# A two-block attention and FFN kernel: a division as its own stage in the second attention, first loads in another order, and slot fills in separate steps

## The chip, the cores and the metric

The kernel runs on one core of a Trainium2 chip. The core has TensorE (PE in the profile; PEld is its weight load, which overlaps the matmuls), VectorE (DVE), ScalarE (ACT), GpSimd (POOL) and SyncE (SP), each with its own instruction queue that runs in order. The engines work on SBUF; PE writes its results to PSUM, from where DVE or ACT copies them to SBUF. The metric is the device time of one execution in microseconds (us), and less is better.

## The reference, cut to what matters

Four layers, each added to x. All is float32; x has 8 x 256 rows of 256, the context 8 x 256 rows of 192.

```python
x = x + _L0_xattn_ref(_layernorm(x), ctx_768, mask, Wq, Wk, Wv, Wo)       # 16 heads of 16
x = x + _L0_ffn_ref(_layernorm(x), gamma, slot_gamma, slot_embeds, w1, b1, w2, b2)
x = x + _L1_xattn_ref(_layernorm(x), ctx_768, w_q, w_k, w_v, w_out, b_out) # 16 heads of 64
x = x + _L1_ffn_ref(_layernorm(x), W_r, W_k, W_v, mu_r, mu_k)

# both attentions: softmax of q k^T over the context's 256 rows, times v, projected back
# _L0_ffn: soft mixture of experts, 8 experts of 128 slots
xn, sn = rmsnorm(x, gamma), rmsnorm(slot_embeds, slot_gamma)
logits = einsum('bnd,esd->bnes', xn, sn)
dispatch, combine = softmax(logits, over n), softmax(logits, over e and s)
slots = einsum('bnd,bnes->besd', xn, dispatch)
out = einsum('bmd,bnm->bnd', gelu(slots @ w1 + b1) @ w2 + b2, combine)
```

## The kernel before, in words

One program builds all instructions in a written order, and a scheduler puts them into the five queues. Matmuls and transposes made through the helpers `matmul` (L73) and `transpose` (L76) keep their written order on PE; other instructions may be moved within their engine. Every dependence becomes a wait on a semaphore. PSUM is split into two large tiles ("big", for scores), three of one bank ("mm", for nearly everything else) and one "o".

**Loads and prologue of the first attention.** ScalarE's queue issues wk, the mask, cq and wq; SyncE's queue issues the first 512 columns of the context (`load_ctx`), x in four pieces of 512 rows (`load_x`), wv, the rest of the context, wo in eight pieces, the slot embeddings `se`, small tensors and the first expert's weights. The landing of a DMA is told by one of eight semaphores in turn, so a DMA can only be issued once the one eight before it has landed. DVE forms `anyk` (does a batch have any key), the two scalars of the key rows, the key rows themselves (`krows`, L280), and the layer-norm statistics of all 16 tiles of x (`ln_pair`, L128 to L132). Then come the first keys (`keys0`), the transposed tokens (`tokens0`) and the first queries (`queries0`).

**First attention.** A loop over 76 steps h: each issues the scores of one query block (for the row maxima, `NM`, L459) and, six steps later, those of one key block (for the exponentials, L470), then whatever a table `whole` holds for that step: keys, values, queries of later batches, `key_rows(p)` at steps 2, 18 and 34, projections, and `slot_sum(e)` at steps 1 to 4, which squares and sums the slot embeddings (`sq` L297, `ssq` L298).

**Routing inside it.** For the first two batches the mixture's routing is also spread over the steps, by two written plans. In a plan "F57.01" means: at step 57 call `fill(0, 1)`, which multiplies the dispatch weights `dt` (kept in the tile `wq`) with x and writes the slots (L717); P, T, U, S, D are the other parts, D being the transposes into `dt`.

**Experts** follow (L933, L949), with the routing of later groups between them.

**Second attention.** 64 steps, one for each batch b and pair of heads t, run in 32 groups of two over "ticks" n. Before, a step has these stages: scores with maxima, exponentials and division (`scores` and `norm`, in one stage), `transposes` of the exponentials (copied to `et`, L1204), `values` (copied to `ot` in every second step, L1223), and at the end of a batch `project` (L1236). `norm` takes the reciprocal of the sums on DVE (L1186) and multiplies on POOL (L1188). The order of a tick is written out:

```python
for n in range(len(groups) + 4):
    b, i = n // 4 + 1, n % 4
    stage(2, n - 3)                     # values
    if b < B:
        for piece in projs[b][1][i]:    # x transposed (i = 0), then queries
            piece()
    stage(3, n - 4)                     # project
    stage(1, n - 2)                     # transposes
    ...                                 # keys (i < 2) or values' projection of a later batch
    stage(0, n)                         # scores and division
```

The queries' copy out of PSUM (`QT`, L1110) and half of that of keys and of values are on DVE, the others on ACT. During the ticks DVE also takes the statistics of the last layer (`ln_half`), and ACT their square root, which needs another function table than the exponentials.

**Last layer**: a pipeline of mix, keys and values over the 8 batches (L1333 and on).

Of the kernel before, what the change touches and what calls it, by code (L numbers as in the profile page):

```python
# [8 lines left out]
F32 = mybir.dt.float32  # L9
# [5 lines left out]
P = 128  # L15
# [47 lines left out]
def kernel(ctx: ExitStack, tc: tile.TileContext, a: dict, out: bass.AP):  # L63
# [38 lines left out]
    make_identity(nc, ident)  # L102
    nc.gpsimd.memset(epsb, EPS)

    def load_x(p):
        nc.sync.dma_start(
            x_sb[:, 4 * p : 4 * p + 4, :],
            a["x"][512 * p : 512 * (p + 1), :].rearrange("(t p) d -> p t d", p=P),
        )

    def ln_half(half, name):
# [8 lines left out]
        nc.vector.reciprocal(rstd, rstd)  # L120
        return mv, rstd

    def ln_pair(p, name):

        mv = stat.tile([P, 4, 2], F32, tag="mvp", bufs=4, name=f"mvp_{name}")
        for i in range(4):
            st = stat.tile([P, 6], F32, tag="bst", bufs=4, name=f"bst_{name}_{i}")
            nc.vector.bn_stats(st, x_sb[:, 4 * p + i, :])  # L128
            nc.vector.bn_aggr(mv[:, i, :], st)
        rstd = stat.tile([P, 4], F32, tag="rstdp", bufs=4, name=f"rstdp_{name}")  # L130
        nc.scalar.activation(rstd, mv[:, :, 1], AF.Sqrt, bias=epsb)
        nc.vector.reciprocal(rstd, rstd)  # L132
        return mv, rstd

    def moe_mean(g):

# [82 lines left out]
    with ExitStack() as l0:  # L219
# [3 lines left out]
        def load_ctx(p):  # L223
# [3 lines left out]
            for h in range(2):  # L227
                nc.sync.dma_start(ctx1T[64 * h : 64 * h + 64, cols], a["ctxT"][P:C, cols])

        wk = w0.tile([P, 2, 512], F32, name="wk")  # L230
        nc.scalar.dma_start(wk[:, 0, :], a["wk0"][0:P, :])
        for h in range(2):
            nc.scalar.dma_start(wk[64 * h : 64 * h + 64, 1, :], a["wk0"][P:C, :])
        load_ctx(0)
        load_x(0)
        maskb = w0.tile([P, B * S], U8, name="maskb")
        nc.scalar.dma_start(maskb, a["mask"].partition_broadcast(P))
        cq = w0.tile([P, 1], F32, name="cq")
        nc.scalar.dma_start(cq, a["cq"])
        wq = w0.tile([P, 2, 512], F32, name="wq")  # L240
        nc.scalar.dma_start(wq, a["wq0"].rearrange("(c p) f -> p c f", p=P))
        wv = w0.tile([P, 2, D], F32, name="wv")
        nc.sync.dma_start(wv[:, 0, :], a["wv0"][0:P, :])
        for h in range(2):
            nc.sync.dma_start(wv[64 * h : 64 * h + 64, 1, :], a["wv0"][P:C, :])
        for p in range(1, 4):
            load_x(p)
        for p in range(1, 4):
            load_ctx(p)

# [1 line left out]
        for j in range(4):  # L252
# [9 lines left out]
        nc.sync.dma_start(b1, a["b1"])  # L262


        nc.vector.tensor_reduce(
            anyk, maskb.rearrange("p (b k) -> p b k", b=B), AX.X, ALU.max
        )


        krows = w0.tile([P, B * S], F32, name="krows")  # L270
        kscale = stat.tile([P, B], F32, tag="kscale", bufs=1, name="kscale")
        kshift = stat.tile([P, B], F32, tag="kshift", bufs=1, name="kshift")
        ones = stat.tile([P, 1], F32, tag="kones", bufs=1, name="kones")
        nc.vector.tensor_reduce(ones, ident[:, HD0 + 1 : P : 32], AX.X, ALU.add)
        nc.vector.tensor_scalar(kscale, anyk, cq, BIG, ALU.mult, ALU.mult)
        nc.vector.tensor_scalar(kshift, kscale, -1.0, ones, ALU.mult, ALU.add)

        def key_rows(p):
            for b in (2 * p, 2 * p + 1):
                nc.vector.tensor_scalar(  # L280
                    krows[:, S * b : S * (b + 1)],
                    maskb[:, S * b : S * (b + 1)],
                    kscale[:, b : b + 1],
                    kshift[:, b : b + 1],
                    ALU.mult,
                    ALU.add,
                )

        key_rows(0)
        qscale = stat.tile([P, B], F32, tag="qscale", bufs=1, name="qscale")  # L290
        nc.vector.tensor_scalar(qscale, anyk, HD0**-0.5, None, ALU.mult)

        ssq = stat.tile([P, E], F32, tag="ssq", bufs=1, name="ssq")

# [98 lines left out]

        def tokens0(b):
            xT = tos[b]["xT"] = p0.tile([P, 2, S], F32, tag="xT", bufs=2, name=f"xT0_{b}")
            mv, rstd = stats0[b // 2]
            pt = transposed(normed(b, mv, rstd, "l0", of=4), f"x0_{b}", transpose)
            nc.scalar.copy(xT, pt)

        def queries0(b, t2):  # L400
# [148 lines left out]
        def at(h, f):  # L549
            whole.setdefault(h, []).append(f)  # L550

        stats0 = [ln_pair(0, "l0_0")]
        tos += [{} for b in range(B)]
        keys0(0, 0)()
        tokens0(0)
        queries0(0, 0)
        at(0, lambda: keys0(0, 1))
        at(1, lambda: queries0(0, 1))
        at(1, lambda: tokens0(1))
# [4 lines left out]
        for p in range(1, 4):  # L564
# [11 lines left out]
            at(h + 15, lambda b=b: queries0(b + 1, 1))  # L576
            at(h + 17, lambda b=b: values0(b))
            at(h + 25, lambda b=b: values0(b + 1))
        stats0 += [ln_pair(p, f"l0_{p}") for p in range(1, 4)]

        for e in range(E):
            at(1 + e // 2, lambda e=e: slot_sum(e))
# [143 lines left out]

        for b, plan in enumerate(
            (
                "P47 T48.00 T49.01 U51.0 T52.10 T53.11 S54.0 U55.1 S55.1 D56.0 F57.00 F57.01 "
                "D58.1 F60.10 F61.11",  # L730
                "P59 T63.00 T64.01 T65.10 U66.0 T68.11 S68.0 U69.1 S69.1 D70.0 F71.00 F72.01 "
                "D73.1 F74.10 F75.11",
            )
        ):
            does = dict(zip("PTUSDF", routing0(b)))
            for step in plan.split():
                when, _, args = step[1:].partition(".")
                at(int(when), lambda f=does[step[0]], args=args: f(*map(int, args)))
# [292 lines left out]
    with ExitStack() as l1:  # L1031
# [116 lines left out]
        def steps1(b, to):  # L1148
# [4 lines left out]
            for t in range(8):  # L1153
# [3 lines left out]
                def scores(t=t, tag=tag, st=st):  # L1157
                    sc = ps_big(f"sc_{tag}").rearrange("p (h q k) -> p h q k", h=2, q=2)
                    for qb in range(2):
                        for i in range(2):  # L1160
                            r = slice(64 * i, 64 * i + 64)
                            matmul(
                                sc[:, i, qb, :],
                                lhsT=to["QT"][r, t, qb * P : (qb + 1) * P],
                                rhs=to["KT"][r, t, b % 2 * S : (b % 2 + 1) * S],
                                start=True,
                                stop=True,
                            )
                    nm = stat.tile([P, 2, 2], F32, tag="nm1", bufs=4, name=f"nm_{tag}")
                    nc.vector.tensor_reduce(nm, sc, AX.X, ALU.max, negate=True)  # L1170
                    ex = p1.tile([P, 2, 2, S], F32, tag="ex", bufs=6, name=f"ex_{tag}")
                    z = stat.tile([P, 2, 2], F32, tag="z1", bufs=4, name=f"z_{tag}")
                    for qb in range(2):
                        for i in range(2):
                            nc.scalar.activation(  # L1175
                                ex[:, i, qb, :],
                                sc[:, i, qb, :],
                                AF.Exp,
                                bias=nm[:, i, qb : qb + 1],
                                accum_out=z[:, i, qb : qb + 1],  # L1180
                            )
                    st["ex"], st["z"] = ex, z

                def norm(tag=tag, st=st):
                    rz = stat.tile([P, 2, 2], F32, tag="rz1", bufs=4, name=f"rz_{tag}")
                    nc.vector.reciprocal(rz, st["z"])  # L1186
                    ex = st["ex"].rearrange("p h q k -> p (h q) k")
                    nc.gpsimd.tensor_tensor(  # L1188
                        ex,
                        ex,  # L1190
                        rz.rearrange("p h q -> p (h q)").unsqueeze(2).to_broadcast([P, 4, S]),
                        ALU.mult,
                    )

                def transposes(tag=tag, st=st):
                    et = p1.tile([P, 2, 2, S], F32, tag="et", bufs=4, name=f"et_{tag}")
                    for i in range(2):
                        pt = ps_mm(f"pe_{tag}_{i}").rearrange("p (c q) -> p c q", c=2)
                        for qb in range(2):
                            for c in range(2):  # L1200
                                transpose(
                                    pt[:, c, qb * P : (qb + 1) * P],
                                    st["ex"][:, i, qb, c * P : (c + 1) * P])
                        nc.vector.tensor_copy(et[:, i, :, :], pt)  # L1204
                    st["et"] = et

                def values(t=t, tag=tag, st=st):
# [29 lines left out]
                        x_sb[:, 2 * b : 2 * b + 2, :], po, x_sb[:, 2 * b : 2 * b + 2, :], ALU.add  # L1237
                    )

                
                def normed_scores(scores=scores, norm=norm):
                    scores()
                    norm()

                steps.append(
                    [normed_scores, transposes, values] + ([project] if t == 7 else [])
                )
            return steps

# [16 lines left out]
                piece()  # L1266
        for n in range(len(groups) + 4):
            b, i = n // 4 + 1, n % 4
            stage(2, n - 3)
            if b < B:  # L1270
                for piece in projs[b][1][i]:
                    piece()
            stage(3, n - 4)
            stage(1, n - 2)


            if i < 2 and n // 8 < B // 2 - 1:
# [165 lines left out]
```

## Time and profile before

| what | us |
|---|---|
| median of 3 runs | 1390.77 (1390.14 to 4721.38) |
| time of the profiled execution | 1386.11 |
| its span, first to last instruction | 1384.2 |
| PE busy | 1324.9 |
| first load of the function table on ACT for the exponentials | 46.6 to 47.9 |
| end of the last attention's projection | about 1326 |

Times in the profile are from the span's start. A group's row has the line, the engine, the operation, output and inputs by their names in the program, shapes and a count; then its busy time, the mean in ns of one, and the idle time of the engine just before them with what ended most of it. A row of the timeline has its start, its duration and the like; the number in brackets is how long the engine was idle before, and what released it. A row of waits has the engine and what it waited for, then the total in us, how often, and the longest. PE's granted clock over the span is 0.990 of full speed; it is lower in the first 25 us, and for some us near 215, 1240 and 1330. DMA moves 86.83 MB, a mean of 63 GB/s.

### The profile page before, as it was taken

Reading aid. Unit: us, or ns where it says so; the run is one execution under the profiler, and the core shown is the slowest. Engines: PE = TensorE matmul, PEld = TensorE weight load, DVE = VectorE, ACT = ScalarE, POOL = GpSimd, SP = SyncE. Lnnn points to the kernel's source line nnn. Section 1 sums busy time; section 2 is a strip of 40 time slices with the busy share of each in tenths; the row PEclk is TensorE's granted clock in tenths of the full one; section 3 lists DMA queues with packets and bytes.
Section 4 is the critical chain, followed back from the end, with each engine's and each line's share of the span. In section 5 each row is a group of like instructions: output and inputs, shape, how many; then the busy total and the mean of one; then the engine's idle time right before and its main releaser. Section 6 shows DMA issues by size and latency. Waiting matters only on the chain.

```text
span 1384.2 us, 18931 instructions
## 1 busy us (share of the span) xinstructions
PE 1324.9 (96%) x7504; PEld 959.3 (69%) x7504; DVE 612.0 (44%) x1223; ACT 543.8 (39%) x1320; POOL 194.9 (14%) x149
## 2 busy tenths in 40 slices
PE   5999998899999999999999999999999999999988
PEld 2566665477778876787867888856666666567667
DVE  6777776523330233322333110036655555655654
ACT  1445453545432262523534232214433433533433
POOL 1000001101010010100101000013332332332414
PEclk8999999999999999999999999999999999999999
DMA  8000000023325231332332435230000000000011
GB/s 259 13 1 1 1 2 1 1 95 130 102 93 193 65 129 65 130 130 76 118 115 79 130 129 168 72 114 0 1 0 1 1 1 0 1 1 1 1 31 54
DMA packets 58375, 86.83 MB, mean 63 GB/s; under 512 B 3248, under 2 KB 47664, under 8 KB 58288
## 3 DMA queue, kind: packets, MB, share of 16 engines
q1 hardware_dynamic: 57424, 84.33, 18.8%
q10 hardware_dynamic: 864, 1.31, 0.3%
q8 instruction: 59, 0.97, 0.3%
q14 instruction: 28, 0.23, 0.1%
HBM read 83.53 MB, written 2.10 MB: 62 GB/s over the span
## 4 chain that ended last, share of the span: by engine, by line
PE 79%; ACT 9%; DVE 7%; issue 2%; POOL 1%; DMA 1%; ACTq 0%; SPq 0%; POOLq 0%; DVEq 0%
PE ph L933 16%; PE pe L949 16%; PE sc L73 7%; ACT ex L1175 6%; PE po L73 5%; PE k L73 5%; PE q L73 4%; PE v L73 4%; PE pc L975 4%; PE o L73 3%; PE pf L879 3%; PE ln L797 3%; PE pe L76 2%; DVE nm L1170 2%; PE pf L73 1%
## 5 line engine op out<-in xcount | busy, mean ns | idle before, releaser
L933 PE MATMUL ph<-slots,w 128*128 128x256 f32 x1024 | 267.6, 385 | 0.8 <-ACT ht L941 0.2
L941 ACT ACTIVATE ht<-ph,b 128x256 f32<-128x256 f32 x256 | 119.2, 474 | 372.3 <-PE ph L933 372.0
L949 PE MATMUL pe<-w,ht 128*128 128x256 f32 x1024 | 263.8, 381 | 0.0
L933 PEld LDWEIGHTS ph<-slots,w 128*128 128x128 f32 x1024 | 182.1, 189 | 55.3 <-ACT ht L941 22.8
L949 PEld LDWEIGHTS pe<-w,ht 128*128 128x128 f32 x1024 | 192.0, 190 | 29.9 <-DVE slots L958 4.2
L1188 POOL TENSOR_TENSOR ex<-ex,rz 128x1024 f32<-128x1024 f32 x64 | 120.0, 1894 | 249.8 <-DVE rz L1186 230.7
L1175 ACT ACTIVATE ex<-sc,nm 128x256 f32<-128x256 f32 x256 | 117.4, 484 | 64.4 <-DVE nm L1170 55.7
L470 ACT ACTIVATE ex<-sc 128x512 f32<-128x512 f32 x128 | 74.8, 597 | 82.9 <-PE sc L73 76.5
L73 PE MATMUL sc<-KT,QT 17*128 17x256 f32 (+1 forms) x1024 | 105.2, 383 | 0.9 <-ACT QT L414 0.9
L958 DVE TENSOR_TENSOR slots<-pe,b 128x512 f32<-128x512 f32 x32 | 22.1, 692 | 183.5 <-PE pe L949 183.5
L459 DVE TENSOR_REDUCE NM<-sc 128x2 f32<-128x512 f32 x128 | 86.8, 688 | 32.7 <-PE sc L73 28.2
L73 PE MATMUL q<-xT,wq 128*128 128x256 f32 x384 | 94.8, 395 | 1.6 <-ACT V L1140 0.9
L73 PEld LDWEIGHTS sc<-KT,QT 17*128 17x128 f32 (+1 forms) x1024 | 78.1, 189 | 23.2 <-issue 13.4
L73 PEld LDWEIGHTS q<-xT,wq 128*128 128x128 f32 x384 | 70.9, 192 | 26.5 <-issue 11.0
L857 POOL TENSOR_TENSOR es<-es,zs 128x1024 f32<-128x1024 f32 x12 | 22.7, 1894 | 445.8 <-DVE zs L856 445.8
L76 PE MATMUL pe<-ident,ex 128*128 128x128 f32 x512 | 70.9, 280 | 13.1 <-DVE QT L1110 9.4
L1204 DVE COPY et<-pe 128x512 f32<-128x512 f32 x128 | 79.8, 677 | 1.9 <-PE pe L76 1.8
L1170 DVE TENSOR_REDUCE nm<-sc 128x4 f32<-128x1024 f32 x64 | 75.3, 1218 | 5.0 <-PE sc L73 1.3
L76 PEld LDWEIGHTS pe<-ident,ex 128*128 128x128 f32 x512 | 56.8, 142 | 27.0 <-POOL ex L1188 11.8
L73 PE MATMUL po<-wo,ot 128*128 128x256 f32 x320 | 72.6, 382 | 0.0
L73 PEld LDWEIGHTS po<-wo,ot 128*128 128x128 f32 x320 | 60.1, 190 | 11.3 <-issue 3.6
L73 PE MATMUL o<-et,V 128*64 128x256 f32 x512 | 62.8, 386 | 0.8 <-ACT ot L1223 0.8
(183 smaller groups left out, 1590.0 us busy)
## 6 DMA issues: line engine op xcount, KB each, us to landing
w<-in_w_dram SPq DMA_DIRECT2D x64, 1024.0 KB, 6.9
b<-in_b_dram SPq DMA_DIRECT2D x32, 128.0 KB, 6.7
x_sb<-in_x_dram SPq DMA_DIRECT2D x4, 512.0 KB, 6.2
out_dram<-y SPq DMA_DIRECT2D x8, 256.0 KB, 2.1
ctx0T<-in_ctxT_dram SPq DMA_DIRECT2D x4, 256.0 KB, 7.4
ctx1T<-in_ctxT_dram SPq DMA_DIRECT2D x8, 128.0 KB, 6.5
se<-in_slots_dram SPq DMA_DIRECT2D x1, 1024.0 KB, 5.7
wq<-in_wq_dram SPq DMA_DIRECT2D x1, 1024.0 KB, 4.8
```

The lines of the kernel that those rows point to most:

```text
L73: tc.keep_in_program_order(nc.tensor.matmul(out, lhsT=lhsT, rhs=rhs, start=start, stop=stop))
L76: tc.keep_in_program_order(nc.tensor.transpose(out, in_, ident))
L459: nc.vector.tensor_reduce(NMs[(2 * b + t // 2) % 2][:, qb, t, HD0 + 1 + 64 * i : 64 * i + 64 : 32], sc[i][:, :, 0, :], AX.X, ALU.max, nega ...
L470: nc.scalar.activation(ex[:, 2 - 2 * i : 4 - 2 * i, :], sc[1 - i][:, :, 1, :], AF.Exp)
L933: nc.tensor.matmul(ph, lhsT=c_["w1"][:, c, hc * P : (hc + 1) * P], rhs=slots[e][:, c * 256 : (c + 1) * 256], start=(c == 0), stop=(c == 1),)
L941: nc.scalar.activation(ht, ph, AF.Gelu, bias=b1[:, e, hc : hc + 1])
L949: nc.tensor.matmul(c_["pe"][:, b, :], lhsT=c_["ht"][hc][:, b * SL : (b + 1) * SL], rhs=c_["w2"][:, hc, :], start=(hc == 0), stop=(hc == HI ...
L975: nc.tensor.matmul(pc[:, :D], lhsT=CT[:, bl, e, t * P : (t + 1) * P], rhs=eos[e][:, bl, :], start=(e == 0), stop=(e == E - 1),)
L1170: nc.vector.tensor_reduce(nm, sc, AX.X, ALU.max, negate=True)
L1175: nc.scalar.activation(ex[:, i, qb, :], sc[:, i, qb, :], AF.Exp, bias=nm[:, i, qb : qb + 1], accum_out=z[:, i, qb : qb + 1],)
L1188: nc.gpsimd.tensor_tensor(ex, ex, rz.rearrange("p h q -> p (h q)").unsqueeze(2).to_broadcast([P, 4, S]), ALU.mult,)
L1204: nc.vector.tensor_copy(et[:, i, :, :], pt)
```

## The change

It has three parts.

In the second attention the division by the sums Z (`norm`) is a stage of its own between scores and transposes: it is written one tick after its scores, behind the transposes of the group before. Of each pair of copies to `et`, the second goes to ACT. The sums have six buffers for four.

The first loads are split and ordered: x comes in two pieces of 256 rows (a new signature of `load_x`), wk and wq in halves of 256 columns, the mask in its first 512 bytes and the rest. A square root is written ahead of them on ACT. The statistics of x are taken for the first 256 rows, then the next 256, then each 512 rows at steps 0, 1 and 2 of the loop (`ln_tiles`); `anyk`, the scalars and the query scale are formed by `key_rows` for two batches at a time. The first tokens are transposed between the two halves of the first keys.

In the plan of the first batch's routing, the second fill goes from step 57 to 58, the second transposes into `dt` from 58 to 60, and the last two fills from 60 and 61 to 61 and 62.

```diff
-    def load_x(p):
+    def load_x(n, of):
         nc.sync.dma_start(
-            x_sb[:, 4 * p : 4 * p + 4, :],
-            a["x"][512 * p : 512 * (p + 1), :].rearrange("(t p) d -> p t d", p=P),
+            x_sb[:, n : n + of, :],
+            a["x"][P * n : P * (n + of), :].rearrange("(t p) d -> p t d", p=P),
         )
-    def ln_pair(p, name):
+    def ln_tiles(n, of, name):
         mv = stat.tile([P, 4, 2], F32, tag="mvp", bufs=4, name=f"mvp_{name}")
-        for i in range(4):
+        for i in range(of):
...
-            nc.vector.bn_stats(st, x_sb[:, 4 * p + i, :])
+            tc.keep_in_program_order(nc.vector.bn_stats(st, x_sb[:, n + i, :]))
             nc.vector.bn_aggr(mv[:, i, :], st)
...
+    def ln_pair(p, name):
+        return ln_tiles(4 * p, 4, name)
...
-        load_ctx(0)
-        load_x(0)
-        nc.scalar.dma_start(maskb, a["mask"].partition_broadcast(P))
+        def load_wk(cols):
+            nc.scalar.dma_start(wk[:, 0, cols], a["wk0"][0:P, cols])
+            for h in range(2):
+                nc.scalar.dma_start(wk[64 * h : 64 * h + 64, 1, cols], a["wk0"][P:C, cols])
+        def load_mask(cols):
+            nc.scalar.dma_start(maskb[:, cols], a["mask"][cols].partition_broadcast(P))
...
+        root = stat.tile([P, 1], F32, tag="rz0", bufs=2, name="root")
+        nc.scalar.activation(root, epsb, AF.Sqrt)
+        load_x(0, 2)
+        load_wk(slice(0, 256))
+        load_ctx(0)
         nc.scalar.dma_start(cq, a["cq"])
-        nc.scalar.dma_start(wq, a["wq0"].rearrange("(c p) f -> p c f", p=P))
+        load_mask(slice(0, 512))
+        load_wq(slice(0, 256))
+        load_x(2, 2)
+        load_wq(slice(256, 512))
+        load_wk(slice(256, 512))
+        load_mask(slice(512, B * S))
...
         def key_rows(p):
+            two, tok = slice(2 * p, 2 * p + 2), slice(512 * p, 512 * (p + 1))
+            tc.keep_in_program_order(
+                nc.vector.tensor_reduce(
+                    anyk[:, two], maskb[:, tok].rearrange("p (b k) -> p b k", b=2), AX.X, ALU.max
+                )
+            )
+            nc.vector.tensor_scalar(kscale[:, two], anyk[:, two], cq, BIG, ALU.mult, ALU.mult)
+            nc.vector.tensor_scalar(kshift[:, two], kscale[:, two], -1.0, ones, ALU.mult, ALU.add)
+            nc.vector.tensor_scalar(qscale[:, two], anyk[:, two], HD0**-0.5, None, ALU.mult)
...
-        stats0 = [ln_pair(0, "l0_0")]
-        keys0(0, 0)()
+        stats0 = [ln_tiles(0, 2, "l0_0")]
+        second = keys0(0, 0)
         tokens0(0)
+        key_rows(0)
+        second()
         queries0(0, 0)
+        stats0 += [ln_tiles(2, 2, "l0_1")]
+        for p in range(1, 4):
+            at(p - 1, lambda p=p: stats0.extend([ln_pair(p, f"l0_{2 * p}")] * 2))
...
-        stats0 += [ln_pair(p, f"l0_{p}") for p in range(1, 4)]
...
-                "P47 T48.00 T49.01 U51.0 T52.10 T53.11 S54.0 U55.1 S55.1 D56.0 F57.00 F57.01 "
-                "D58.1 F60.10 F61.11",
+                "P47 T48.00 T49.01 U51.0 T52.10 T53.11 S54.0 U55.1 S55.1 D56.0 F57.00 F58.01 "
+                "D60.1 F61.10 F62.11",
...
-                    z = stat.tile([P, 2, 2], F32, tag="z1", bufs=4, name=f"z_{tag}")
+                    z = stat.tile([P, 2, 2], F32, tag="z1", bufs=6, name=f"z_{tag}")
...
-                    nc.vector.reciprocal(rz, st["z"])
+                    tc.keep_in_program_order(nc.vector.reciprocal(rz, st["z"]))
...
-                        nc.vector.tensor_copy(et[:, i, :, :], pt)
+                        (nc.scalar.copy if i else nc.vector.tensor_copy)(et[:, i, :, :], pt)
...
-                def normed_scores(scores=scores, norm=norm):
-                    scores()
-                    norm()
                 steps.append(
-                    [normed_scores, transposes, values] + ([project] if t == 7 else [])
+                    [scores, norm, transposes, values] + ([project] if t == 7 else [])
                 )
...
-            stage(2, n - 3)
+            stage(3, n - 3)
...
-            stage(3, n - 4)
-            stage(1, n - 2)
+            stage(4, n - 4)
+            stage(2, n - 2)
+            stage(1, n - 1)
```

## The prediction

> **What bounds the kernel now.** I read the engine shares first, then busy time by stage, then the waits and the gaps of TensorE (PE).
>
> ```profile
> PE 1324.9 (96%) x7504; PEld 959.3 (69%) x7504; DVE 612.0 (44%) x1223; ACT 543.8 (39%) x1320; POOL 194.9 (14%) x149
> ```
>
> ```profile
> 0.00:46.00 46.00, 30.52 (x132) 16.02 (x136) 32.22 (x98) 7.33 (x14) 3.57 (x13) 0.89 0.70 204
> 46.00:260.00 214.00, 203.57 (x1900) 125.80 (x1900) 153.12 (x310) 109.57 (x206) 13.39 (x17) 0.98 0.01 1
> 260.00:925.00 665.00, 660.06 (x2964) 511.13 (x2958) 171.09 (x377) 245.63 (x474) 31.31 (x21) 1.00 0.34 111
> 925.00:1322.00 397.00, 380.01 (x2279) 262.36 (x2278) 224.18 (x376) 157.25 (x577) 127.50 (x74) 1.00 0.00 1
> ```
>
> The rows by stage are busy times of PE, PEld, DVE, ACT, POOL, then clock, DMA share, GB/s. PE is the bound: only its idle 59 us, and its work at reduced clock, can be won. The change adds and removes no matmul. It reaches 15.5 us of idle at the start, some of the 10.4 us in the first attention, and the 17 us of the second.
>
> ```profile
> PE pe L76 <- DVE QT L1110: 9.4, 13, 2.2
> ...
> PE pe L76 <- DVE et L1204: 3.0, 4, 1.3
> PE k L73 <- DVE et L1204: 2.3, 4, 0.6
> ```
>
> ```profile
> 1034.14 0.51 ACT L1175 ACTIVATE ex<-sc,nm 128x256 f32<-128x256 f32 x1
> ...
> 1034.59 0.62 ACT L1223 COPY ot<-o 128x512 f32<-128x512 f32 x1
> 1034.84 0.18 DVE L1186 RECIPROCAL rz<-z 128x4 f32<-128x4 f32 x1 [1.65 <-ACT ex L1175]
> 1034.94 0.66 DVE L1110 TENSOR_SCALAR QT<-q 128x512 f32<-128x512 f32 x1
> ...
> 1035.74 1.16 PE L76 MATMUL pe<-ident,ex 128*128 128x128 f32 x8 [0.61 <-DVE QT L1110]
> ```
>
> The reader is to see a queue: DVE's reciprocal waits for the last exponential, QT's copy stands behind it, and the transposes wait for that copy, since q and the transposes share the three "mm" PSUM buffers.
>
> **Second attention: division as its own stage.** The reciprocal moves one tick later, behind the transposes' copies, and half of these (64 of 128) go from DVE to ACT. The reciprocal no longer waits, since its exponentials are a tick old. I count a tick from the start of values (at 1030.38). In ticks with one query piece, QT's copy can run from 3.9 to 4.6 instead of ending at 5.2, so the third transpose group finds its buffer free. The keys need the buffer of the second group, which ACT now empties: exponentials to 4.2, ot to 4.85, copy 0.6, free at 5.45, needed at 5.95. The eleven gaps of 0.61 and the first of 0.51 go: 7.2 us. In ticks that begin with pt_x, PE is at the keys by 4.6 already and ACT's copy still ends at 5.45: the four gaps of 0.57 become some 0.8, which loses 0.9. The gap at 1240 (2.17) goes with its half-speed work after it (transposes 1.75 for 1.16, scores 2.94 for 1.89): 3.8. The late gaps 0.54, 0.57, 0.56, where a copy stood behind the same reciprocal, go: 1.7. The 0.79 behind ot stays.
>
> One place gets worse: tick 20 (from 1174.8), where the FFN statistics put a square root between exponentials.
>
> ```profile
> 1176.04 1.28 ACT L1175 ACT_TABLE_LOAD   x1 [2.26 <-DVE nm L1170]
> ...
> 1180.18 0.66 PE L76 MATMUL pe<-ident,ex 128*128 128x128 f32 x4 [1.32 <-DVE et L1204]
> ...
> 1181.90 2.02 DVE L173 TENSOR_SCALAR xh_ffn<-x_sb,mv_ffn,rstd_ffn 128x256 f32<-128x256 f32 x2
> ```
>
> The exponentials there end 1.9 late, and ACT's copies stand behind them; the normalization of x (xh_ffn) now comes ahead of the V copy and the maxima. I get some 0.6 later maxima, exponentials to 1181.5, ot 1182.1, copy 1182.7, so keys start 2.0 later than their 1180.8. PE then idles some 3.3 us. Does the clock fall? The Trainium skill, "TensorE: Matmul & The Clock Gate", "HAM oscillation — how this bites in real kernels", wants no gap over about 3.4 us: by it this gap and that of 1240 cost nothing more. The trace disagrees: after 2.17 us the granted clock was 0.66 over 1240 to 1245. I take the trace: another 1.6 lost. Second attention: 7.2 + 3.8 + 1.7 - 0.9 - 2.0 - 1.6 = 8.2 us gained (by the page, at tick 20: 9.8).
>
> A second rule speaks against the move. POOL's multiplication (1894 ns, two a tick) now runs from about 5 to 9 of a tick, where half of each xh stands. Of two xh_ffn beside it, one took 1693 ns against a usual 0.4. The skill's "SBUF — State Buffer", "SBUF: two separate sides", says DVE in a two-port mode and GpSimd exclude each other for a whole instruction. So up to 1.9 us of DVE per such tick; DVE's next work there, the keys' copy, begins at 9.0, so I cost it at nothing. Without that cover the maxima and ACT would be late by as much; that is the slow rival. POOL's order also gets x + bias between two multiplications; at 5.9 us per tick in the shortest ticks its 3.8 us still fit. At the tail the last division comes some 0.9 later (POOL done at 1315.3 for 1314.4), and the second transposes start then: 0 to 0.2, taken as nothing.
>
> **First loads.** Now DVE does mask, all 16 statistics and 8 key rows before the first scores:
>
> ```profile
> 10.34 2.29 DVE L265 TENSOR_REDUCE anyk<-maskb 128x8 f32<-128x2048 uint8 x1 [10.34 <-DMA maskb<-in_mask_dram]
> ...
> 24.36 0.42 SPq L259 DMA_DIRECT2D se<-in_slots_dram  x1
> ...
> 25.65 0.71 PE L73 MATMUL sc<-KT,QT 17*128 17x256 f32 x8 [0.87 <-ACT QT L414]
> ...
> 31.36 0.75 DVE L297 TENSOR_TENSOR sq<-se 128x256 f32<-128x256 f32 x2
> ```
>
> Afterwards: x's first 256 KB land near 4.7, keys run on a cold PE (3.8 + 2.1 us by the rows at 6.01 and 9.73), the 64 KB mask waits for x's landing and comes near 10 (cq, 0.5 KB, took 4.7), key rows to 12, KT to 13.3, q and QT: first scores about 16 to 17, nine earlier. But this does not carry through. DVE then has maxima 1.3, statistics of four tiles 2.0 (0.4 + 0.17 each, a little overlapped), maxima 1.3, KT 1.2, statistics 2.0, maxima 1.3, and reaches the slot embeddings' squares (sq) near 26 to 27. Their load landed at 30.1 before (24.36 + 5.7). In DVE's new order sq still stands ahead of the second step's maxima, so the early scores wait there. The split loads put 39 DMAs ahead of it instead of 33, over eight landing semaphores; the bytes ahead are the same and the DMA engines were full (share above 1 from 5 to 20 us), so I set the landing to 31 (29 to 33). SP is moved past one more x load, ACT past five more issues of about 0.5 us; ACT has idle time there, and its table load is hidden under the first DMAs.
>
> From there to the transposes of the third x block: squares and sums 5.3, the last four statistics 1.6, maxima 3 x 1.2, mask and key rows of the second pair 1.6, QT 0.6, KT 1.2, xh 0.7, so 14.5, and 0.5 for a PE that has cooled: 46.0 against 45.27 before. A loss of 0.8, with ends of +4 (load before 26.5) and -3 (load at 33). Key rows of the third and fourth pairs, formerly in the prologue, stand in DVE's queue at steps 18 and 34, 1.8 us each (0.57 + 0.5 + 0.7), ahead of the next maxima that PE needs: between 0 and 1.8 each, I take 0.4 each: -0.8.
>
> **Slots filled in separate steps.** The rows at 222.54 (PE waits 1.31 for a slots copy) and 227.25 (0.45 for ACT's V copy) are from two fills in one step and transposes placed next to them. The new order puts scores and v between: both go, +1.8. The half-speed stretch at 213 to 219 comes from gaps before it (0.46, 0.62, 1.04, 0.24) that stay.
>
> **The sum.** 8.2 - 0.8 - 0.8 + 1.8 = 8.4 us, made against a span of 1384.2. The profiled execution took 1386.1, 4.7 below the median 1390.8 of the runs; carried to that median: 1382.4.
>
> **Rivals.** (a) The start counts: slot embeddings land before DVE wants them, and ACT keeps up in tick 20. Start +4 instead of -0.8, tick 20 without its 3.6: 1374. For it: DMA delivers up to 360 GB/s; against: the unchanged bytes ahead. (b) Nothing gained: load at 33, clock falls in two or three more gaps at 1.6 each, since the gate depends on where gaps lie: 1388 to 1391. (c) Slower: ACT becomes the bound of the copies. Its margin is 0.5 us (5.45 against 5.95); it decides as soon as maxima and exponentials come over 0.5 late, for which a DVE instruction held by POOL is enough. With 1.0 late in every tick: gaps of 0.5 in the eleven ticks (gain only 1.2), 1.8 in the four that begin with pt_x and have keys (-4.9), half of these with a fallen clock (-3.2), tick 20 -4, 1240 and the late gaps +5.5, a late load and the rest -2: 7.4 lost, 1398. With 1.9 late in each (gaps of 1.4 and 2.7, a fallen clock in all four): near 1416. For it: xh_ffn's 1693 ns; against: the cover above. (d) The change does nothing as it says: excluded by the instruction order, in which the reciprocal does move.
>
> **How the numbers follow.** Forecast 0.50 (1377 to 1387), (a) 0.27, (b) 0.13, (c) 0.10. The predicted time is the forecast's, 1382. From 1369 to 1394: below lie the better end of (a), above half of (c) and more. Over 2%, which is about what a measurement of this kernel can tell from no change, means below 1363 or above 1418.6. Below 1363 needs 28 us of some 34 within reach (17 + 1.6 in the second attention, about 12 at the start, 3.5 at the slots): 0.07 with what I may have missed. Above: the worst end of (c) and a little more, 0.03. Within: 0.90.
>
> **What would show it.** In the profile after: no wait of pe on QT; pe and the second copy on ACT; a gap ahead of k on ACT's et in pt_x ticks near 0.8, and one of about 3 us at the square root; first scores near 17, then DVE waiting for se near 27 to 31; no wait of pf on slots. Wrong, if DVE never waits for se, or if PE waits on ACT in the ticks with query pieces.

## The result, and the profile after

| | before | after |
|---|---|---|
| median, first pair of runs | 1390.45 (1387.64 to 4721.38, 4 runs) | 1375.62 (1375.34 to 1376.09, 4 runs) |
| median, repeated on another chip (e5 below) | 1387.86 (1384.71 to 1393.16, 27 runs) | 1374.75 (1373.91 to 1377.28, 6 runs) |
| profiled execution: time, span | 1386.11, 1384.2 | 1375.81, 1373.9 |

The ratio is 0.990 (95% interval 0.9881 to 0.992), and 0.9903 (0.9883 to 0.9924) in the repetition: 13 to 15 us faster, about 1%. That is under the 2% that count as a difference here, though both intervals lie clear of 1, and 6.4 us below the predicted 1382. The run of 4721 us stands alone and enters no ratio. The profiled execution of the kernel before was 4.3 us faster than its median, so the spans differ by less than the medians.

First the busy shares in the page of the kernel after, and its busy times by stage (PE, PEld, DVE, ACT, POOL, then clock, DMA share, GB/s):

```profile
PE 1326.6 (97%) x7504; PEld 961.3 (70%) x7504; DVE 575.1 (42%) x1172; ACT 578.9 (42%) x1386; POOL 194.6 (14%) x149
```

```profile
0.00:46.00 46.00, 32.27 (x121) 16.05 (x122) 29.68 (x89) 7.11 (x15) 3.56 (x13) 0.85 0.70 204
46.00:260.00 214.00, 204.33 (x1889) 125.66 (x1889) 156.99 (x328) 109.02 (x205) 12.71 (x16) 0.98 0.01 1
260.00:925.00 665.00, 660.60 (x2973) 513.63 (x2974) 170.51 (x379) 245.77 (x475) 31.90 (x22) 1.00 0.34 111
925.00:1322.00 397.00, 382.70 (x2312) 265.53 (x2310) 192.18 (x330) 195.24 (x648) 127.52 (x76) 1.00 0.01 3
```

PE is busy 1.75 us more in the first 46 us than before, but at a mean clock of 0.85 instead of 0.89: part of what it gained there is work at half speed (from 30 to 33 and from 37 to 43 us, among others). These means are not safe, though: over the first 12 us the profile states 1.00 in both, while the first key matmuls, which run then, take 3.8 us for the 2.0 of the next ones. DVE is busy 37 us less over the whole kernel and ACT 35 us more, and neither is near its limit. Fixed windows hide where time is won, because the work slides through them. So I use marks, the same event in both traces:

| mark (start of the instruction) | before | after | after, repeated | gained |
|---|---|---|---|---|
| first scores | 25.65 | 18.09 | 18.81 | 7.6, 6.8 |
| third x transposes | 45.27 | 46.90 | 46.07 | -1.6, -0.8 |
| first residual add (`x_sb<-po`) | 88.98 | 92.78 | 91.94 | -3.8, -3.0 |
| last add of the mixture (`x_sb<-pc`) | 909.99 | 912.90 | 911.08 | -2.9, -1.1 |
| last add of the second attention | 1326.03 | 1315.17 | 1313.37 | 10.9, 12.7 |

A head start of 7 us is gone 28 us later, and the second attention (from the fourth mark to the fifth) then wins 13.8 us in both executions. Its waits in the kernel after (engine and what it waited for, us in total, times, longest):

```profile
PE k L73 <- ACT et L1235: 5.1, 5, 1.7
PE o L73 <- ACT ot L1254: 0.9, 1, 0.9
PE q L73 <- ACT V L1171: 0.9, 1, 0.9
PE v L73 <- ACT et L1235: 0.8, 1, 0.8
...
```

No transpose waits for the query copy any more (9.4 us before). Instead the matmuls of keys and values wait 5.9 us for the copies that went to ACT (before, the keys waited 2.3 us for copies on DVE). At the start, rows of DVE's timeline and then of PE's (start, duration, then in brackets how long the engine stood and for what):

```profile
27.48 0.66 DVE L486 TENSOR_REDUCE NM<-sc 128x2 f32<-128x512 f32 x1
31.25 0.76 DVE L323 TENSOR_TENSOR sq<-se 128x256 f32<-128x256 f32 x2 [3.11 <-DMA se<-in_slots_dram]
```

```profile
36.21 0.77 PE L73 MATMUL sc<-KT,QT 17*128 17x256 f32 x4 [3.36 <-DVE NM L486]
37.47 1.22 PE L73 MATMUL sc<-KT,QT 17*128 17x256 f32 x4 [0.49 <-DVE NM L486]
38.62 1.12 PE L76 MATMUL nm<-ident,NM 128*128 128x128 f32 x4
39.53 1.06 PE L73 MATMUL k<-ctx0T,wk 128*128 128x512 f32 x1
```

And from PE's waits over the first 75 us:

```profile
PE sc L73 <- DVE NM L486: 4.8, 3, 3.4
```

DVE comes to the squares of the slot embeddings at 28 and stands for their load. Behind that instruction in its queue are the row maxima, and PE's scores wait 3.36 us for those. PE's rows after it show a second price: `nm` takes 1.12 us for a usual 0.66, because the clock has fallen.

### The profile page after: what moved, and what is told of

Its sections match the earlier page's. It is cut to its first block, busy times and chain, and to the rows that moved or that the text cites. A ratio compares the mean times of both kernels' runs of the same rounds, so it can differ in the third digit from the quotient of the medians.

```text
span 1373.9 us, 19006 instructions
## 1 busy us (share of the span) xinstructions
PE 1326.6 (97%) x7504; PEld 961.3 (70%) x7504; DVE 575.1 (42%) x1172; ACT 578.9 (42%) x1386; POOL 194.6 (14%) x149
## 3 DMA queue, kind: packets, MB, share of 16 engines
q1 hardware_dynamic: 57440, 84.33, 18.8%
q10 hardware_dynamic: 1584, 1.31, 0.4%
## 4 chain that ended last, share of the span: by engine, by line
PE 84%; ACT 6%; DVE 4%; DMA 2%; issue 2%; POOL 1%; SPq 0%; POOLq 0%; ACTq 0%; DVEq 0%
PE ph L964 16%; PE pe L980 15%; PE sc L73 8%; PE q L73 6%; PE o L73 5%; PE po L73 5%; PE k L73 5%; PE pc L1006 4%; PE v L73 4%; PE pe L76 4%; PE ln L828 3%; PE pf L910 3%; ACT ex L1206 2%; PE pf L73 1%; ACT ex L497 1%
## 5 line engine op out<-in xcount | busy, mean ns | idle before, releaser
L1235 ACT COPY et<-pe 128x512 f32<-128x512 f32 x64 | 37.0, 607 | 71.9 <-PE pe L76 71.5
```

## The experiments

Each experiment's median stands beside the kernel before on the same chip: 1387.16 for e1 to e4, 1387.86 for e5 to e8, 1387.19 for e9 to e12. On one chip they can be compared directly, between chips by their ratio to the kernel before.

**The parts alone (e1, e2, e3).** The kernel before with one part of the diff each: e1 the hunks of the second attention, e2 those of the loads, first statistics and key rows, e3 the routing plan.

> Before, with the second attention of the change alone (division as a stage of its own, the second copy of each pair on ScalarE, z with six buffers). Theory: all of the gain lies here and the second attention was undervalued in the prediction (8.2 us): the time falls by about 14 us, to some 1376 to 1377, below the changed kernel or level with it, and the marks of the batches' ends come 49.7 us apart instead of 51.5. Rival, the prediction's own sum: 8.2 us here, and the rest of the 14.8 us between the medians from elsewhere: 1382.

> Before, with the loads, first statistics and key rows of the change alone. Theory: the first scores start 7.5 us earlier but VectorE then stands 3 us for the slots' embeddings and TensorE's clock falls, so that nothing of the head start is left: slower than before by 3 to 4 us, about 1394. Rival (the prediction's rival a): the early start counts and something else in the changed kernel hides it: faster by 3 to 7 us, 1384 to 1387.

> Before, with the changed plan of the slots' fills alone. Theory: one wait goes (1.3 us) and another of scores for ScalarE comes, so 0 to 0.8 us faster. Rival, the prediction's sum: 1.8 us faster, if the new wait came with the later arrival at this stage and not from the plan.

Measured: e1 1375.91, ratio 0.9922 (0.9907 to 0.9937); e2 1388.87, 1.0012 (1.0001 to 1.0022); e3 1385.29, 0.999 (0.998 to 1.0). The second attention carries the gain: its stretch takes 401.8 us in e1, for 416.0 before and 402.3 after. The loads alone lose 1.7 us, half of what was expected. The plan alone wins 1.9, by the marks 1.84 at the end of the mixture. There my new theory fell and the prediction's number was right: from the first residual add to the first expert matmul the first profile of after wins only 0.4 us, but the clock over 260 to 300 us is 0.96 there; in the repetition (1.00) it wins 1.7 against e2, which has the same loads and the old plan. Over all 14 profiles of this document, from the first residual add to the end of the mixture, the six with the old plan take 820.8 to 822.3 us and the eight with the new one 819.1 to 820.2.

**Is the whole more than its parts (e5)?** The kernel after again, unchanged.

> The changed kernel as it is, beside the three below and the kernel before on one chip, because the three parts measured alone add up to about 11 us and the whole to 14.8 of medians (10.3 of spans). Theory: the parts add up and the whole is worth 11 us, a ratio of about 0.992. Rival: the parts help each other, and the ratio is again 0.990 or less.

The parts sum to 11.4 us by their medians, the whole is 13.1 here. The intervals (about 3 us) hold both, so I see no help between the parts, but a difference of 2 us could not be seen.

**The two halves of the second attention (e6, e7).** e6 has the stage of its own, e7 the copies on ACT:

```diff
 # e6: e1 with
-    (nc.scalar.copy if i else nc.vector.tensor_copy)(et[:, i, :, :], pt)
+    nc.vector.tensor_copy(et[:, i, :, :], pt)
 # e7: before with
-    nc.vector.tensor_copy(et[:, i, :, :], pt)
+    (nc.scalar.copy if i else nc.vector.tensor_copy)(et[:, i, :, :], pt)
```

> Before, with the division as a stage of its own (and six buffers of z), but both copies of each pair on VectorE as before. Theory: it is the moved reciprocal that pays, since VectorE's in-order queue stood in it for ScalarE's sums and held the copies and query copies behind it: 8 to 11 us faster, of the 11 us that both parts bring. Rival: VectorE's load is what pays (0.69 us of copy for each pair), and the stage alone brings 0 to 3 us.

> Before, with the second copy of each pair on ScalarE, but the division still behind the scores as before. Theory (the moved reciprocal pays): at most 3 us faster, or slower, because each copy on ScalarE lengthens the queue whose sums VectorE stands for. Rival (VectorE's load pays): 7 to 11 us faster.

Measured: e6 1372.19, ratio 0.9884 (0.9861 to 0.9908); e7 1385.28, 0.998 (0.9971 to 0.9989). The moved reciprocal pays, with 15.7 us even more than the 8 to 11 expected (it comes with the six buffers of the sums, which were not tried apart). Unexpected is that it pays more alone. All of PE's waits of e6 in the stretch of the second attention, and past it one of the last layer:

```profile
PE pk L1329 <- DVE xk L1315: 5.9, 1, 5.9
PE pe L76 <- POOL ex L1188: 1.6, 4, 0.8
PE q L73 <- ACT V L1140: 0.9, 1, 0.9
PE o L73 <- ACT ot L1223: 0.8, 1, 0.8
PE pe L76 <- DVE xT L1090: 0.5, 1, 0.5
```

No wait for any copy of `et` is left, though DVE makes them all; the waits for POOL's products are in the last two batches. By the marks, the copies on ACT cost and bring, on top of the stage:

| us | before | e7 copies | e6 stage | after: both |
|---|---|---|---|---|
| first batch, from the last add of the mixture | 103.79 | 103.60 | 101.32 | 102.81 |
| each of batches 1 to 3 | 51.47 | 50.95 | 49.50 | 49.71 |
| batch 4 (tick 20, feed-forward statistics) | 52.15 | 54.05 | 49.99 | 51.60 |
| batch 5 (the gap at 1240) | 48.36 | 47.28 | 43.93 | 43.52 |
| batches 6 and 7 | 57.34 | 55.64 | 57.15 | 55.21 |
| last add of the mixture to last add here | 416.0 | 413.4 | 400.9 | 402.3 |

On top of the stage they win 1.9 us at the tail and 0.4 in batch 5, and lose these and 1.4 more before: 1.5 in the first batch, 0.6 in the next three, 1.6 in batch 4. By the times alone e1 and e6 just touch in their intervals, but the marks repeat: the stretch takes 400.9 to 401.1 us in the four profiles that have the stage with all copies on DVE (e6, e9, e10, e12), and 401.8 to 403.7 in the six that have it with half of them on ACT.

**Slot sums later (e4).**

```diff
-    at(1 + e // 2, lambda e=e: slot_sum(e))
-at(5, slot_scale)
+    at(6 + e, lambda e=e: slot_sum(e))
+at(14, slot_scale)
```

> The changed kernel, with the sums of squares of the slots' embeddings at steps 6 to 13 instead of 1 to 4 and their roots at step 14 instead of 5, so that VectorE never stands for that load. Theory (VectorE's in-order queue behind this load gave the head start back): the third x transposes start some 4 to 7 us before 46.9 us, the clock between 30 and 45 us stays above .9, and the time falls by 4 to 7 us, to 1369 to 1372. Rival: another wait holds the same stretch (ScalarE's table change, the mask rows, the wait for the second half of the loads): within 1.5 us of the changed kernel.

Measured: 1374.28, ratio 0.9912 (0.9893 to 0.9931): no gain, as the rival had it. DVE still stood 1.3 us for the load, since the scheduler put the first square at 31.0. The third x transposes did come at 42.4, but the squares ended at 45.9, and their root then stood in ACT's queue with a table load behind it, ahead of the first exponentials. ACT's rows and PE's:

```profile
45.97 0.21 ACT L328 ACTIVATE ssq<-ssq 128x8 f32<-128x8 f32 x1 [2.20 <-DVE ssq L324]
46.20 1.28 ACT L497 ACT_TABLE_LOAD   x1
```

```profile
48.95 0.93 PE L73 MATMUL sc<-QT,KT 18*128 18x256 f32 x8 [2.92 <-ACT ex L497]
49.64 1.09 PE L73 MATMUL sc<-KT,QT 17*128 17x256 f32 x8
50.66 3.78 PE L73 MATMUL q<-xT,wq 128*128 128x256 f32 x8
```

Of the 4.5 us won, 2.92 turned into this wait, and in the profiled execution (1381.64; the others took 1373.2 to 1374.7) the clock stayed at half for 18 us after it, though PE was at work all along: the same query matmuls take 1.99 us at full clock. What took the rest in the other executions can't be seen, since they were not profiled.

**Slot sums on ACT (e8).** In the kernel after, ACT has nothing to do from 36.6 to 42.9 us but wait for these sums.

```diff
-    nc.vector.tensor_tensor(sq[:, 0, :], se[:, e, :], se[:, e, :], ALU.mult)
-    nc.vector.tensor_reduce(ssq[:, e : e + 1], sq[:, 0, :], AX.X, ALU.add)
+    tc.keep_in_program_order(nc.scalar.activation(
+        sq[:, 0, :], se[:, e, :], AF.Square, accum_out=ssq[:, e : e + 1]))
...
-    at(1 + e // 2, lambda e=e: slot_sum(e))
-at(5, slot_scale)
+    at(3, lambda e=e: slot_sum(e))
+at(4, slot_scale)
```

The root in `slot_scale` is kept in written order too.

> The changed kernel, with the squares of the slots' embeddings summed by ScalarE (Square with an accumulated sum, all eight at step 3, their roots at step 4) instead of by two VectorE instructions each, so that VectorE neither stands for that load nor works 6.5 us on it, and the roots are done before the first exponential. Theory: the third x transposes at 41 to 43 us instead of 46.9, no wait of the scores for VectorE over 1.5 us and none for ScalarE's exponential over 2 us before 70 us, and 4 to 6 us faster than the changed kernel on the same chip: about 1370 to 1372. Rival: the head start is lost elsewhere (a fall of the clock after other short waits): within 1.5 us of the changed kernel.

Measured: 1366.68, ratio 0.9844 (0.9819 to 0.9868), 8 us under the kernel after on the same chip, more than the 4 to 6 expected. The third x transposes start at 41.37. PE's waits in the first 75 us of e8:

```profile
...
PE sc L73 <- ACT ex L500: 2.1, 3, 1.4
PE sc L73 <- ACT QT L444: 1.5, 1, 1.5
PE sc L73 <- DVE NM L489: 0.9, 1, 0.9
```

The wait for maxima fell from 4.8 to 0.9 us. The first residual add is at 85.35, 6.6 us ahead of e5.

**The slot load earlier (e11).** The kernel after, with the load of `se` ahead of the contexts 1 to 3.

```diff
+        se = w0.tile([P, E, D], F32, name="se")
+        nc.sync.dma_start(se, a["slots"].rearrange("e s d -> s e d"))
         for p in range(1, 4):
             load_ctx(p)
```

> The changed kernel with the load of the slots' embeddings issued ahead of the contexts 1 to 3 and of wo, nothing else moved. Theory (half of the loss is VectorE standing 3 us for that load, half its 6.5 us of work on it): VectorE does not stand before the first square, the third x transposes come at about 43 to 44 us, and it is 2 to 4 us faster than the changed kernel, about 1371. Rival: the work alone counts, or the contexts arrive too late for the second keys: no faster than the changed kernel.

Measured: 1371.84, ratio 0.9892 (0.9875 to 0.9908); its interval and that of the kernel after overlap. The edit did not take the standing away: the scheduler put the first squares further forward, and DVE stood longer and earlier.

```profile
17.14 0.73 DVE L177 TENSOR_SCALAR xh_l<-x_sb,mvp_l,rstdp_l 128x256 f32<-128x256 f32 x2
21.82 0.76 DVE L323 TENSOR_TENSOR sq<-se 128x256 f32<-128x256 f32 x2 [3.94 <-DMA se<-in_slots_dram]
```

The third x transposes came at 44.71, 1.4 us ahead of e5, but the clock then fell for some 7 us (from 63 us), and the first residual add is at 92.0, as in the kernel after. So it leaves open how the loss divides between standing and 6.5 us of work.

**The best of it, and two parts taken back (e9, e10, e12).** e9 is e8 with all copies of `et` on DVE; e10 is e9 with the old loads, first statistics and key rows, e12 is e9 with the old plan.

> The changed kernel with the squares summed by ScalarE (as in the run before) and with both copies of each pair back on VectorE: the stage of the division and the loads stay. Theory (ScalarE's copies are a loss once the reciprocal has moved): the wait of the key and value matmuls for ScalarE's copy (5.6 us) goes, the batches' ends stand 49.5 us apart, 50.0 in the batch with the feed-forward statistics, and the time is 1362 to 1364. Rival: it is as fast as with the copies on ScalarE, 1366 to 1368.

> The kernel of e9 with the loads, first statistics and key rows of the kernel before. Theory: the first scores 7.5 us earlier count once VectorE is relieved, so this is slower than e9 by 3 to 6 us, about 1367. Rival: what the sums on ScalarE brought is VectorE's 6.5 us of work alone, and the loads are worth nothing: within 1.5 us of e9.

> The kernel of e9 with the plan of the slots' fills of the kernel before. Theory: the plan brings what it brought alone, so this is 1 to 2 us slower than e9. Rival: in the changed kernel the plan brought 0.6 us (a new wait for ScalarE's exponential took the rest), so within 0.8 us of e9.

Measured: e9 1365.2 (1364.15 to 1365.68), ratio 0.9838 (0.9825 to 0.9851), which beats both kernels: 22 us under before, some 9 under after. e10 1370.96, 0.988; e12 1368.11, 0.9858. The loads are thus worth 5.8 us of medians here (3.5 by the mark at the end of the mixture; their intervals don't meet), the plan 2.9 (1.9 by that mark; these intervals do meet). The copies back on DVE can't be judged by the times: e9's and e8's ratios can't be told apart. e9 lies between its theory and its rival: against e8 the second attention takes 401.1 for 403.7 us, of which 1.7 is a fall of the clock in e8's batch 4, and the first residual adds are level, since e8's fall of the clock at 28 us is the longer one and e9 has another at 59 us.

The first residual add gives a square of four for loads and sums:

| first residual add at, us | sums on DVE | sums on ACT |
|---|---|---|
| old loads | 88.98, 88.80 (e3), 88.71 (e6); 90.92 (e1), 92.47 (e7) | 88.53 (e10) |
| new loads | 92.78, 91.94 (e5), 91.98 (e2), 92.00 (e11) | 85.35 (e8), 85.62 (e9), 85.47 (e12) |

In e1 and e7 the clock rose later; beside the three other profiles, and with one profile of e10, it does not matter with the old loads who sums. With the new ones it is worth over 6 us: they win 3 us if DVE is free at that time, and lose 3 if it isn't. That the new loads win with the sums on ACT stands on the times too (e9 against e10); the loss without them is 1.7 us by the medians of e2, and by these marks no larger than the spread of the old start. (e4 is left out: 99.37, with its 18 us at half clock.)

## Why the prediction was right or wrong

The time lies in the range, and the mechanisms that the prediction named are in the trace, but three terms were off and the errors partly cancelled. It lies below the 1377 to 1387 in which the forecast had its half of the chance, and within 2 us of rival (a)'s 1374; that is luck, since that rival's start did not come true. On the profiles of before and e5:

| step | predicted | measured |
|---|---|---|
| second attention | +8.2 | +13.8 |
| start, up to the first residual add | -0.8 | -2.7 (-3.0 by the mark, less the key rows in it) |
| key rows at steps 18 and 34 | -0.8 | -0.5 |
| slots | +1.8 | +1.7 |
| the rest of the mixture, and the last layer | 0 | 0.0 (+0.4, -0.5) |
| sum, on a span of 1384.2 | 8.4 | 12.2 |

In the first profile of after the sum is 10.3.

- **Second attention: the mechanism was right, the size was not.** The gaps that the step counted lie in the batches like this:

| batch | predicted | measured |
|---|---|---|
| first | +1.5 | +1.0 |
| 1 to 3, each | +1.0 | +1.8 |
| 4, with tick 20 | -2.4 | +0.5 |
| 5, with the gap at 1240 | +4.4 | +4.8 |
| 6 and 7 | +1.7 | +2.1 |

The largest error is tick 20, put at -3.6 with its fallen clock. PE idled there 0.42, 0.26 and 1.71 us, 2.4 for the old 1.3, which loses 1.1 where the step said 2.0; and the clock did not fall in that execution, so the 1.6 was not paid. That is 2.5 us. The next is batches 1 to 3. Each has two of the gaps of 0.61 and one tick with pt_x (0.23 lost), which makes 1.0; the marks show 1.76. A tick with a query piece, in PE's rows before and then after:

```profile
1034.09 1.04 PE L76 MATMUL pe<-ident,ex 128*128 128x128 f32 x8
1035.74 1.16 PE L76 MATMUL pe<-ident,ex 128*128 128x128 f32 x8 [0.61 <-DVE QT L1110]
1036.85 1.98 PE L73 MATMUL k<-ctx0T,wk 128*128 128x512 f32 x4
1038.76 1.13 PE L73 MATMUL k<-ctx1T,wk 64*128 64x512 f32 x4
```

```profile
1035.90 2.20 PE L76 MATMUL pe<-ident,ex 128*128 128x128 f32 x16
1037.94 1.88 PE L73 MATMUL k<-ctx0T,wk 128*128 128x512 f32 x4
1039.75 1.13 PE L73 MATMUL k<-ctx1T,wk 64*128 64x512 f32 x4
```

From the first row to the last are 4.67 and 3.85 us: the tick won 0.82 where the row of the gap says 0.61, because the matmuls beside the gap are shorter too. The same holds for the first values of a batch (0.2 won with no gap), and the tick with pt_x lost 0.08 for 0.23. The first batch won less than its step, for the reason in the next point.
- **The split of the copies was credited wrongly.** The step said that the keys need the buffer "which ACT now empties". The gap in the ticks that begin with pt_x came as computed (0.77 for 0.8). But e6 shows that the same keys find their buffer free when DVE empties it, once the reciprocal is out of its way. On balance the copies cost about 1.4 us; they gain only in the last three batches. The prediction's own sign of being wrong, PE waiting on ACT in a tick with query pieces, came true once, in the first batch:

```profile
955.39 1.98 PE L73 MATMUL v<-wv,ctx0T 128*128 128x512 f32 x4 [0.76 <-ACT et L1235]
```

In e6 this wait is not there. So rival (c), ACT as the bound of the copies, named the right danger: it happens in the ticks without slack, and is too small to decide.
- **Start: right up to the third transposes, then short.** Scores at 16 to 17 were forecast and came at 18.1 (e5: 18.8). DVE's standing for the slot load was forecast near 27 to 31 and is in the row at 31.25. The third transposes were forecast at 46.0 and came at 46.08 in e2 and 46.07 in e5 (46.90 in the first profile). What no step had is 2 us between there and the first residual add: the clock fell again after a wait of 1.41 us that was there before and cost nothing more then (last section). Rival (a) was not real for this kernel, but e8 makes it real with one edit: its condition, that DVE need not wait for the slot embeddings, was the right one.
- **POOL beside DVE** cost what the step said outside tick 20, nothing: no `xh_l` of the second attention took over 0.41 us. In tick 20 one `xh_ffn` took 1.77 us and the maxima behind it came later, which is in the gap of 1.71. The fear of 1.9 us per tick was not idle: in e6, where DVE keeps all copies, three `xh_l` and one `xh_ffn` that start beside POOL's multiplications take 1.98 us each. No gap of PE follows them, so the cover that the step counted on held.
- **Key rows** cost about 0.25 us for 0.4: from the first to the third residual add, around step 34, are 51.77 us for 51.51; step 18 lies ahead of the first add and is put at the same. **Slots** came out right as a number: e3 gives 1.84, e12 1.9, by the mark at the end of the mixture. The two waits of 1.31 and 0.45 went, as the step said, but scores now wait 0.67 us for an exponential behind them (e3, and 0.68 in after), which no step had; the 0.24 that the step left standing goes in e3 and e5.

## What to carry to other kernels

On an engine that runs its queue in order, look first for the one instruction that waits, and only then for work to take away: here a reciprocal one tick later was worth 15 us, while taking half of the copies off the same engine was worth 2.6 alone and cost 1.4 on top. An earlier start can be worth nothing until every in-order queue on its way is looked through for an instruction that still waits for a late load; here eight squares on another, idle engine turned a small loss into a gain of 3 us or more. Marks of the same event in two traces show what rows of waits and fixed windows hide.

## What the runs showed of the hardware that was not expected

**The same wait can cost its length or about twice that.** In the first attention PE waits 1.41 us for exponentials in every one of these kernels (1.42 in e4), with the same matmuls around it. PE's rows in the kernel before, then after:

```profile
63.57 0.76 PE L73 MATMUL sc<-QT,KT 18*128 18x256 f32 x8 [1.41 <-ACT ex L470]
64.11 0.66 PE L73 MATMUL sc<-KT,QT 17*128 17x256 f32 x8
64.70 0.66 PE L76 MATMUL nm<-ident,NM 128*128 128x128 f32 x4
```

```profile
65.42 0.76 PE L73 MATMUL sc<-QT,KT 18*128 18x256 f32 x8 [1.41 <-ACT ex L497]
65.96 0.66 PE L73 MATMUL sc<-KT,QT 17*128 17x256 f32 x8
66.55 0.66 PE L76 MATMUL nm<-ident,NM 128*128 128x128 f32 x4
```

Busy times and clock of the five us behind it, before and then after:

```profile
68.00:73.00 5.00, 5.00 (x48) 3.01 (x48) 3.27 (x6) 2.60 (x5) 0.00 (x0) 1.00 0.01 3
```

```profile
68.00:73.00 5.00, 5.00 (x25) 1.93 (x24) 1.90 (x4) 1.18 (x2) 0.00 (x0) 0.71 0.01 3
```

In six of the 14 profiles (before, e1, e3, e6, e8, e10) the clock stays at 1.00 and the key matmuls behind the wait take 1.88 us; in the other eight they take 2.9 to 3.6, some 1.0 to 1.7 us more for nothing that differs near it. It fell in one of six profiles with the old loads and in seven of eight with the new ones, which suggests that what comes earlier has a part in it. Tick 20 shows the reverse: here the kernel after keeps its clock and e8 does not. The keys behind its gap in after, then in e8 with the five us from there:

```profile
1179.37 1.13 PE L73 MATMUL k<-ctx0T,wk 128*128 128x512 f32 x2 [1.71 <-ACT et L1235]
1180.42 1.13 PE L73 MATMUL k<-ctx1T,wk 64*128 64x512 f32 x4
```

```profile
1170.64 1.13 PE L73 MATMUL k<-ctx0T,wk 128*128 128x512 f32 x2 [1.72 <-ACT et L1238]
1171.70 1.98 PE L73 MATMUL k<-ctx1T,wk 64*128 64x512 f32 x4
1170.00:1175.00 5.00, 4.36 (x14) 2.34 (x16) 0.96 (x2) 1.66 (x4) 2.02 (x2) 0.68 0.00 0
```

After's clock is 1.00 over the five us from 1179, and e1, e4, e5 and e11 keep theirs too. e8's batch 4 takes 53.30 us for 51.60.

So neither the prediction's flat 1.6 us for each such gap nor nothing is right: the outcome changes with an edit elsewhere. The Trainium skill, "TensorE: Matmul & The Clock Gate", Part 1, says that the gate watches free-running windows of about 3.4 us, so that the first rise comes earlier or later from run to run; if the same holds for a gap, its place in a window matters. These pairs agree with that but do not show it. The page's rule that the clock falls after at least one idle window of that length does not fit single gaps of 1.41 us, in eight profiles. What decides was not tried.

**The clock's first rise varies too.** Kernels with the same start had full clock from about 25 us (e6) or from 29 to 30 us (e7, e1): the key matmuls at 26 us took 1.98 us in e6, 3.24 in e7 and 3.73 in e1, and the first residual add came 2.2 us later in e1 and 3.8 in e7 (which also had the fall behind the 1.41 us). Such differences may make most of the spread of the kernel before (1384.7 to 1393.2 in 27 runs), but that is not shown, since only one execution of it is profiled. A gain of 2 us cannot be read from one profile.
